# Flamingo kernel on one core: weight loads in another order, and the attentions' output bias added one tile at a time

## The chip, the core and the metric

The kernel runs on one core of a Trainium2 chip. The core has five engines that run at the same time, each with its own queue of instructions served in order: TensorE (PE in the profile; its weight loads are PEld), VectorE (DVE), ScalarE (ACT), GpSimd (POOL) and SyncE (SP), which here only issues DMAs. Engines wait for one another through semaphores. The metric is the device time of one execution in microseconds (us); lower is better.

## The reference

The input x has 2 batches of 2048 tokens with 512 features. A context of 2 x 128 tokens with 384 features is attended to. There are two layers, each a gated cross-attention and a gated feed-forward:

```python
def cross(x, y):                # 16 heads, over 128 context tokens
    q, k, v = proj(x), proj(y), proj(y)
    return softmax(q @ k.T * scale) @ v @ Wo + bo
x = x + tanh(g_xattn[0]) * cross0(layernorm(x), ctx)     # biased, inner width 512
x = x + tanh(g_ffn[0])   * routed(layernorm(x))
x = x + tanh(g_xattn[1]) * cross1(layernorm(x), ctx)     # inner width 1024
x = x + tanh(g_ffn[1])   * ternary_conv_ffn(layernorm(x))
```

`routed` picks the 256 tokens of each batch with the highest scores, runs causal attention and a SiLU-gated feed-forward of width 1365 on them, and writes them back. `ternary_conv_ffn` quantizes activations to integers and weights to -1, 0, 1, goes to width 2048, convolves over three neighbouring tokens, applies SiLU, quantizes again and projects back to 512.

## The kernel before

Everything is unrolled. The order of instructions on each engine is made by a planner: it takes the program's order as a priority and places what its own clock says is ready, so a later, ready instruction can pass an earlier one that waits. An instruction under `tc.keep_in_program_order` is kept where the program has it. Within a queue the order is then fixed, and an instruction that waits holds all behind it.

**Start.** ScalarE's queue issues the loads of bk, the first four x tiles (`load_x(0, nc.scalar)`, L989) and bq. SP's queue issues, in `load_context` (L160 to L168), the context ctxT, the key weights wk, the query weights wq, the value weights wv and bv, and then in `load_rest` (L172 to L174) the output weights wo and bias bo, which VectorE scales by the gate; then w_router and eight more x tiles. TensorE makes keys (L182) and values (L201), VectorE adds their biases (L191, L210), and then the first block's tokens are normalized (L104), transposed (L113) and projected to queries (L253).

**Stage 1** (L0 cross-attention) works on 8 blocks of 512 tokens. A block has 16 units, one head each: scores (L276), row maximum (L119, VectorE), exponent (L122, ScalarE), reciprocal (L130), the product with it (L131, POOL), transposes of the probabilities (L294), and values (L302) once per four heads. The output projection `back` of a block is cut into eight pieces, one per unit of the following block: a half of a tile's matmuls pp (L320), then the other half and L329, a VectorE operation that adds the gated pp to the residual tile and so frees pp's PSUM buffer. Ahead of the first piece POOL adds the bias bo to all four residual tiles (L316), so L329 need not wait for bias later. Beside the units run the router's scores and ranks (L810, L862, L906, VectorE).

**Stage 2** works on the selected tokens of one batch after the other: selected attention and then `feed_forward`, in 11 chunks of 128 columns. For each chunk SP loads w1c, w2c and w3c (L619 to L627), three chunks ahead, and TensorE makes pu, pw (L648) and acc (L633). Beside it weights are made ternary (`ternary`; L731 stores w2b). The second cross-attention's weights are loaded by the same `load_context` after the first batch's feed-forward in the program, and by `load_rest` in the third piece of the second batch's selected attention; its keys and values are made beside that attention.

**Stage 3** (L1 cross-attention) has 8 blocks of 16 units like stage 1 and runs beside the convolution of the blocks before: matmuls ph (L1159), POOL's small copies (L1169, L1171), VectorE's L1170, ScalarE's L1172 and two VectorE L1176 with two SBUF operands per slice. The end projects the quantized integers (L1389) and stores the output; the stores are issued on POOL's queue except those of the last block.

Of the kernel before, what the change touches and what calls it, by code (L numbers as in the profile page):

```python
# [17 lines left out]
P = 128  # L18
# [4 lines left out]
TB = BLK // P  # L23
# [7 lines left out]
NF = (DFF + P - 1) // P  # L31
# [7 lines left out]
def row_tiles(ap):  # L39
    return ap.rearrange("(c p) n -> p c n", p=P)  # L40
# [3 lines left out]
def flamingo_kernel(ctx: ExitStack, tc: tile.TileContext, a: dict, out: bass.AP):  # L44
    nc = tc.nc
# [4 lines left out]
    def psum_pool(stack, name, bufs):  # L50
        return stack.enter_context(tc.tile_pool(name=name, bufs=bufs, space=PSUM))
# [87 lines left out]
    class CrossWeights:  # L139
# [12 lines left out]
                self.bq = w.tile([P, nE], F32, name=L + "bq")  # L152
                self.bk = w.tile([P, nE], F32, name=L + "bk")

        def load_context(self, st, side):

            L, E = self.L, self.nE * P
            wkv = st.enter_context(tc.tile_pool(name=L + "wkv", bufs=1, side=side))
            self.ctxT = wkv.tile([P, CC, B * M], F32, name=L + "ctxT")
            nc.sync.dma_start(out=self.ctxT, in_=row_tiles(a["ctxT"]))  # L160
            self.wk = wkv.tile([P, CC, E], F32, name=L + "wk")
            nc.sync.dma_start(out=self.wk, in_=row_tiles(a[L + "WkT"]))
            nc.sync.dma_start(out=self.wq, in_=row_tiles(a[L + "WqT"]))
            self.wv = wkv.tile([P, CC, E], F32, name=L + "wv")
            nc.sync.dma_start(out=self.wv, in_=row_tiles(a[L + "WvT"]))
            if self.bias:
                self.bv = wkv.tile([P, E], F32, name=L + "bv")
                nc.sync.dma_start(out=self.bv, in_=a[L + "bv"].partition_broadcast(P))  # L168

        def load_rest(self):  # L170
            L = self.L
            nc.sync.dma_start(out=self.wo, in_=row_tiles(a[L + "WoT"]))  # L172
            nc.sync.dma_start(out=self.bo, in_=a[L + "bo"].partition_broadcast(P))
            nc.vector.tensor_scalar(self.bo, self.bo, self.g, None, ALU.mult)  # L174
# [40 lines left out]
    def cross_attention(  # L215
# [8 lines left out]
        L, nE, bias = W.L, W.nE, W.bias  # L224
        E = nE * P
# [86 lines left out]
        def back(n, residual, OT):  # L312

            tiles = residual()
            for t in tiles:
                tc.keep_in_program_order(nc.gpsimd.tensor_tensor(t, t, W.bo, ALU.add))  # L316
            for i, t in enumerate(tiles):
                pp = ps_mm.tile([P, D], F32, name="pp", tag="mm")
                for e in range(nE):
                    nc.tensor.matmul(  # L320
                        pp,
                        OT[e][:, ts(i, P)],
                        W.wo[:, e, :],
                        start=(e == 0),
                        stop=(e == nE - 1),
                    )
                    if e == nE // 2 - 1:
                        yield
                nc.vector.scalar_tensor_tensor(t, pp, W.g, t, ALU.mult, ALU.add)  # L329
                if i == TB - 1:  # L330
                    after_block(n, tiles)
                yield
# [10 lines left out]
        for U in range(N * H + 12):  # L343
            n, u = divmod(U, H)
            if n < N:
                grp, t = divmod(u, 4)
# [18 lines left out]
            if 0 <= V < N * H and V % 4 == 3:  # L365
                n, grp = divmod(V // 4, 4)
# [240 lines left out]
        yield from rms_rows(rows, g2, h2T[b], mm, pool)  # L607

    AHEAD = 3

    def feed_forward(b, ps_acc, mm, work):

        w13, gT = {}, {}
        acc = [ps_acc.tile([P, D], F32, name=f"acc{i}", tag=f"acc{i}") for i in range(2)]

        def load(f):
            n = min(P, DFF - f * P)
            w1c = wst.tile([P, DC, P], F32, name="w1c", tag="w1c")
            nc.sync.dma_start(  # L619
                out=w1c[:, :, :n], in_=row_tiles(a["W1T"])[:, :, ds(f * P, n)]  # L620
            )
            w2c = wst.tile([P, DC, P], F32, name="w2c", tag="w2c")
            nc.sync.dma_start(
                out=w2c[:, :, :n], in_=row_tiles(a["W2T"])[:, :, ds(f * P, n)]
            )
            w3c = wst.tile([P, D], F32, name="w3c", tag="w3c")
            nc.sync.dma_start(out=w3c[:n, :], in_=a["W3T"][ds(f * P, n), :])  # L627
            w13[f] = (w1c, w2c, w3c)

        def down(f):  # L630
            n = min(P, DFF - f * P)
            for i in range(2):
                nc.tensor.matmul(  # L633
                    acc[i],
                    gT[f][:n, ts(i, P)],
                    w13[f][2][:n, :],
                    start=(f == 0),
                    stop=(f == NF - 1),
                )

        for f in range(AHEAD):
            load(f)
        for f in range(NF):
            n = min(P, DFF - f * P)
            pu, pw = mm([P, CAP], "pu"), mm([P, CAP], "pw")
            for pt, wt in ((pu, w13[f][0]), (pw, w13[f][1])):
                for d in range(DC):
                    nc.tensor.matmul(  # L648
                        pt[:n, :],
                        wt[:, d, :n],  # L650
                        h2T[b][:, d, :],
                        start=(d == 0),
                        stop=(d == DC - 1),
                    )
            su = fact.tile([P, CAP], F32, name="su", tag="su")
            nc.scalar.activation(su[:n, :], pu[:n, :], AF.Silu)
            gT[f] = fact.tile([P, CAP], F32, name="gT", tag="gT")
            nc.vector.tensor_tensor(gT[f][:n, :], pw[:n, :], su[:n, :], ALU.mult)
            if f > 0:
                down(f - 1)  # L660
                if f - 1 + AHEAD < NF:
                    load(f - 1 + AHEAD)
            for w, n in work:
                for _ in range(n):
                    next(w, None)
        down(NF - 1)
        for w, _ in work:
            for _ in w:
                pass

        for i in range(2):
            t = xa[2 * b + i]
            nc.vector.tensor_tensor(t, acc[i], t, ALU.add)
            nc.vector.tensor_scalar(t, t, gf[0], None, ALU.mult)
            nc.gpsimd.indirect_dma_start(
                out=x_d[b][:, :],
                out_offset=bass.IndirectOffsetOnAxis(
                    ap=idx[:, 2 * b + i : 2 * b + i + 1], axis=0
                ),
                in_=t,  # L680
                in_offset=None,
                compute_op=ALU.add,
            )
# [61 lines left out]
    with ExitStack() as st:  # L745
# [16 lines left out]
            out=pick,  # L762
            in_=pick,
# [10 lines left out]
            out=after,  # L774
# [8 lines left out]
        def load_x(n, queue=nc.sync):  # L783
            if n < B * NBLK:
                for t in range(n * TB, (n + 1) * TB):
                    x[t] = xres.tile([P, D], F32, name="x", tag="x")
                    queue.dma_start(out=x[t], in_=x_in[t])
# [198 lines left out]
        sel_pools = selected_pools(st)  # L986
        W0 = CrossWeights("L0_", D // P, True, gx[0], st, "left")
        nc.scalar.dma_start(out=W0.bk, in_=a["L0_bk"])
        load_x(0, nc.scalar)  # L989
        nc.scalar.dma_start(out=W0.bq, in_=a["L0_bq"])  # L990
        with ExitStack() as st0:
            W0.load_context(st0, "left")
            W0.load_rest()
            nc.sync.dma_start(out=w_router, in_=a["w_router"].partition_broadcast(P))
            nc.vector.tensor_reduce(w_sum, w_router, AX.X, ALU.add)
            for n in (1, 2):
                load_x(n)
            selected_constants()
            with ExitStack() as st1:
                for _ in W0.keys_values(in_pool(psum_pool(st1, "L0_ps0", 2), "kv")):  # L1000
                    pass
# [41 lines left out]
    w4 = right.enter_context(tc.tile_pool(name="w4", bufs=1, side="right"))  # L1043
    w1q = w4.tile([P, DC, HID], BF16, name="w1q")
    W1 = CrossWeights("L1_", 1024 // P, False, gx[1], right1, "right")
    W1.load_context(right2, "right")
    with ExitStack() as sp:
        ps_o = psum_pool(sp, "s2b_o", 2)
        ps_sc = psum_pool(sp, "s2b_sc", 4)
        mm = in_pool(psum_pool(sp, "s2b_mm", 2), "mm")  # L1050
        second = selected_attention(
            1, mm, in_pool(ps_sc, "sc"), in_pool(ps_o, "o"), 4, selected_pools(sp), 2
        )
        keys_values = W1.keys_values(mm)
        for k, _ in enumerate(second):
            if k == 2:
                W1.load_rest()
            if k % 3 == 1:
                next(keys_values, None)
        for _ in keys_values:  # L1060
            pass
    with ExitStack() as sp:
        mm = in_pool(psum_pool(sp, "s2c_mm", 6), "mm")
        raw = raw_pools(sp)
        feed_forward(1, psum_pool(sp, "s2c_acc", 1), mm, [(ternary(0, mm, *raw), 1)])
    nc.vector.tensor_scalar(finstep, step[:, 1:2], gf[1], None, ALU.mult)
    sf.close()
    s2.close()
# [454 lines left out]
```

## Time and profile before

| what | value |
|---|---|
| median of 3 runs | 1771.91 us (1771.09 to 1772.97) |
| the profiled execution | 1771.65 us |
| its span, first to last instruction | 1770.0 us |
| mean granted TensorE clock | 0.971 |
| TensorE busy, first stretch 30 to 550 us | 473.5 of 520 us |
| TensorE busy, stage 3, 780 to 1600 us | 783.4 of 820 us |
| first matmul starts at | 11.02 us |
| L316, bias adds on POOL | 64, 86.8 us together |
| L131, products on POOL | 256, 275.8 us together |

Rows of the list of waits read: engine, tile and line that waited, who ended the wait, us in total, times, longest. Rows of the timeline read: start, duration, engine, line, operation, out<-in, shape, count, and in brackets the engine's idle time before it and what ended it. Where several instructions are merged, the duration is that of the row. Rows of the windows read: the stretch, its length, the busy time of PE, PEld, DVE, ACT and POOL with counts, the granted TensorE clock, the DMA engines' busy share and GB/s.

### The profile page before, as it was taken

Reading aid. Unit: us, or ns where it says so; the run is one execution under the profiler, and the core shown is the slowest. Engines: PE = TensorE matmul, PEld = TensorE weight load, DVE = VectorE, ACT = ScalarE, POOL = GpSimd, SP = SyncE. Lnnn points to the kernel's source line nnn. Section 1 sums busy time; section 2 is a strip of 40 time slices with the busy share of each in tenths; the row PEclk is TensorE's granted clock in tenths of the full one; section 3 lists DMA queues with packets and bytes.
Section 4 is the critical chain, followed back from the end, with each engine's and each line's share of the span. In section 5 each row is a group of like instructions: output and inputs, shape, how many; then the busy total and the mean of one; then the engine's idle time right before and its main releaser. Section 6 shows DMA issues by size and latency. Waiting matters only on the chain.

```text
span 1770.0 us, 25204 instructions
## 1 busy us (share of the span) xinstructions
PE 1642.2 (93%) x8076; PEld 863.0 (49%) x8122; DVE 1251.5 (71%) x2576; ACT 1101.4 (62%) x3170; POOL 556.4 (31%) x703
## 2 busy tenths in 40 slices
PE   6999889989999988999999999999999999989988
PEld 3544444445555655755454544545444454434433
DVE  4566877865757543345358888799788878877986
ACT  2876566456563323435367878778777787765575
POOL 2534443442440021023224242242423424233121
PEclk9999999999899989999999999999999999989999
DMA  6021112121006870730011334234143233247384
GB/s 218 7 67 55 36 61 66 51 75 54 25 36 207 286 241 25 229 87 25 19 54 72 109 110 146 90 114 155 42 158 117 84 104 118 88 161 269 135 305 153
DMA packets 116171, 196.98 MB, mean 111 GB/s; under 512 B 13084, under 2 KB 50716, under 8 KB 112328
## 3 DMA queue, kind: packets, MB, share of 16 engines
q1 hardware_dynamic: 109288, 176.50, 29.2%
q0 software_dynamic: 5888, 17.83, 3.2%
q8 instruction: 64, 1.05, 0.2%
q10 hardware_dynamic: 864, 1.05, 0.2%
q14 instruction: 67, 0.55, 0.1%
HBM read 120.89 MB, written 74.45 MB: 110 GB/s over the span
## 4 chain that ended last, share of the span: by engine, by line
PE 28%; DVE 18%; ACT 4%; DMA 3%; issue 2%; POOL 1%; SPq 0%; DVEq 0%; POOLq 0%; ACTq 0%
PE pq L253 8%; PE pp L320 7%; DVE h L1176 5%; PE po L302 3%; PE sc L276 3%; PE ph L1159 3%; PE tp L294 2%; DVE u L1170 2%; DVE nmx L119 1%; PE po L1389 1%; DVE AT L295 1%; DMA hf<-h_d 1%; DVE hf L1259 1%; ACT A L122 1%; DVE h L1209 1%
## 5 line engine op out<-in xcount | busy, mean ns | idle before, releaser
L122 ACT ACTIVATE A<-sc,nmx 128x128 f32<-128x128 f32 x1024 | 363.8, 385 | 130.1 <-DVE nmx L119 121.0
L131 POOL TENSOR_TENSOR A<-A,rden 128x512 f32<-128x512 f32 x256 | 275.8, 1079 | 510.2 <-DVE rden L130 407.6
L320 PE MATMUL pp<-L_wo,OT 128*128 128x512 f32 x768 | 367.0, 609 | 11.8 <-DVE x L329 11.7
L253 PE MATMUL pq<-xnT,L_wq 128*128 128x512 f32 x768 | 347.2, 600 | 12.1 <-DVE x L329 12.1
L122 ACT ACTIVATION_READ_ACCUMULATOR A<-sc,nmx 128x1 f32 x1024 | 229.5, 224 | 0.0
L253 PEld LDWEIGHTS pq<-xnT,L_wq 128*128 128x128 f32 x768 | 143.4, 192 | 172.7 <-issue 152.1
L119 DVE TENSOR_REDUCE nmx<-sc 128x4 f32<-128x512 f32 x256 | 168.6, 678 | 74.4 <-PE sc L276 74.3
L320 PEld LDWEIGHTS pp<-L_wo,OT 128*128 128x128 f32 x768 | 136.5, 193 | 157.6 <-issue 133.2
L1176 DVE SCALAR_TENSOR_TENSOR h<-u,cw,h 128x512 f32<-128x512 f32 x256 | 206.1, 838 | 6.1 <-ACT h L1172 5.6
L294 PE MATMUL tp<-ident,A 128*128 128x128 f32 x1024 | 164.7, 285 | 19.1 <-POOL A L131 13.9
L294 PEld LDWEIGHTS tp<-ident,A 128*128 128x128 f32 x1024 | 118.9, 143 | 88.3 <-issue 41.0
L295 DVE COPY AT<-tp 128x512 f32<-128x512 f32 x192 | 129.7, 677 | 44.4 <-PE tp L294 43.9
L276 PEld LDWEIGHTS sc<-L_kT,qT 32*128 32x128 f32 (+1 forms) x2048 | 110.7, 193 | 72.1 <-issue 60.3
L1172 ACT ACTIVATE h<-u,cb,cw 128x512 f32<-128x512 f32 x128 | 99.2, 808 | 68.6 <-DVE u L1170 57.5
L276 PE MATMUL sc<-L_kT,qT 32*128 32x128 f32 (+1 forms) x2048 | 136.9, 294 | 4.0 <-ACT A L122 3.4
L302 PE MATMUL po<-AT,L_v 128*32 128x512 f32 (+1 forms) x512 | 121.6, 667 | 11.5 <-DVE AT L295 11.0
L1159 PE MATMUL ph<-xiT,w1q 128*128 128x512 bf16 x477 | 122.7, 379 | 4.1 <-DVE u L1170 2.2
L1389 PE MATMUL po<-w2q,hq 128*128 128x512 bf16 x501 | 116.6, 380 | 9.3 <-ACT hq L1369 5.1
L1170 DVE TENSOR_TENSOR u<-ph,inv_b 128x512 f32<-128x512 f32 x128 | 85.4, 683 | 32.4 <-PE ph L1159 28.3
L130 DVE RECIPROCAL rden<-den 128x4 f32<-128x4 f32 x256 | 43.2, 169 | 80.2 <-ACT A L122 73.0
L1169 POOL COPY u<-carry 128x2 f32<-128x2 f32 x112 | 42.8, 384 | 147.0 <-DVE h L1176 121.8
L1159 PEld LDWEIGHTS <-w1q 128*128 128x128 bf16 x512 | 49.2, 98 | 81.2 <-issue 37.6
(246 smaller groups left out, 2389.2 us busy)
## 6 DMA issues: line engine op xcount, KB each, us to landing
h_d<-h SPq DMA_DIRECT2D x28, 1024.0 KB, 3.9
x_d<-x SPq DMA_DIRECT2D x64, 256.0 KB, 2.0
hf<-h_d SPq DMA_DIRECT2D x64, 256.0 KB, 3.2
x<-h_d SPq DMA_DIRECT2D x48, 256.0 KB, 4.7
x_d<-xo SPq DMA_DIRECT2D x32, 256.0 KB, 2.5
xf<-x_d SPq DMA_DIRECT2D x32, 256.0 KB, 3.1
x<-x_d SPq DMA_DIRECT2D x32, 256.0 KB, 3.0
hq_d<-hi SPq DMA_DIRECT2D x64, 128.0 KB, 1.8
```

What stands on the lines that cost most here:

```text
L119: nc.vector.tensor_reduce(nmx, sc, AX.X, ALU.max, negate=True)
L122: nc.scalar.activation(out_tile[:, h, :], sc[:, h, :], AF.Exp, bias=nmx[:, h : h + 1], accum_out=den[:, h : h + 1],)
L131: nc.gpsimd.tensor_tensor(out_tile, out_tile, rden.unsqueeze(2).to_broadcast([P, n, width]), ALU.mult,)
L253: nc.tensor.matmul(pq, W.wq[:, d, ts(e, P)], xnT[:, d, :], start=(d == 0), stop=(d == DC - 1),)
L276: nc.tensor.matmul(sc[h][:, t, :], qT[e % cpg][r, ts(t, P)], W.kT[r, b, e, :], start=True, stop=True,)
L294: nc.tensor.transpose(tp[:, t, :], A[:, t, :], ident)
L295: copy(AT, tp.rearrange("p t n -> p (t n)"))
L302: nc.tensor.matmul(po[h * dh : (h + 1) * dh, :], W.v[:, b, ts(hd, dh)], AT[c * hpc + h], start=True, stop=True,)
L320: nc.tensor.matmul(pp, OT[e][:, ts(i, P)], W.wo[:, e, :], start=(e == 0), stop=(e == nE - 1),)
L1159: nc.tensor.matmul(ph, w1q[:, d, ts(c, P)], xiT[g][:, d, :], start=(d == 0), stop=(d == DC - 1),)
L1176: nc.vector.scalar_tensor_tensor(z, u[:, ds(k, BLK)], cw[:, c, k : k + 1], z, ALU.mult, ALU.add)
L1389: nc.tensor.matmul(po, rows(c), w2q[:, c, :], start=(c == 0), stop=(c == HC - 1))
```

## The change

In both cross-attentions `load_context` and `load_rest` become one generator, `load_keys`, with two stops. It issues ctxT and wk, wk in two halves; then wv; then wq, bv, wo and bo. For layer 0 the first four x tiles are loaded on SP's queue between the second part and the third, no longer on ScalarE's. For layer 1 each part is tied by `issue_after` to a load of the feed-forward on SP's queue, and can't be issued ahead of it: ctxT and wk behind w3c of batch 0's last but one chunk, wv behind that of its last chunk, the rest behind w3c of batch 1's chunk 5 (counted from 0). In `back` the bias is added to the first tile at the front, and to tile i+1 after the stop in the middle of tile i's matmuls.

```diff
-        def load_context(self, st, side):
+        def load_keys(self, st, side):
             self.ctxT = wkv.tile([P, CC, B * M], F32, name=L + "ctxT")
             nc.sync.dma_start(out=self.ctxT, in_=row_tiles(a["ctxT"]))
             self.wk = wkv.tile([P, CC, E], F32, name=L + "wk")
-            nc.sync.dma_start(out=self.wk, in_=row_tiles(a[L + "WkT"]))
-            nc.sync.dma_start(out=self.wq, in_=row_tiles(a[L + "WqT"]))
+            for k in range(2):
+                half = ts(k, E // 2)
+                nc.sync.dma_start(
+                    out=self.wk[:, :, half], in_=row_tiles(a[L + "WkT"])[:, :, half]
+                )
+            yield
             self.wv = wkv.tile([P, CC, E], F32, name=L + "wv")
             nc.sync.dma_start(out=self.wv, in_=row_tiles(a[L + "WvT"]))
+            yield
+            nc.sync.dma_start(out=self.wq, in_=row_tiles(a[L + "WqT"]))
...
-        def load_rest(self):
-            L = self.L
             nc.sync.dma_start(out=self.wo, in_=row_tiles(a[L + "WoT"]))
...
             tiles = residual()
-            for t in tiles:
+            def add_bias(i):
+                t = tiles[i]
                 tc.keep_in_program_order(nc.gpsimd.tensor_tensor(t, t, W.bo, ALU.add))
+            add_bias(0)
             for i, t in enumerate(tiles):
...
                     if e == nE // 2 - 1:
                         yield
+                        if i + 1 < TB:
+                            add_bias(i + 1)
...
+            issued[b, f] = nc.sync.dma_start(out=w3c[:n, :], in_=a["W3T"][ds(f * P, n), :]).ins
...
-        load_x(0, nc.scalar)
...
-            W0.load_context(st0, "left")
-            W0.load_rest()
+            loads = W0.load_keys(st0, "left")
+            next(loads)
+            next(loads)
+            load_x(0)
+            for _ in loads:
+                pass
...
-    W1.load_context(right2, "right")
+    loads = W1.load_keys(right2, "right")
+    with tc.issue_after(issued[0, NF - 2]):
+        next(loads)
...
-            if k == 2:
-                W1.load_rest()
+            if k == 0:
+                with tc.issue_after(issued[0, NF - 1]):
+                    next(loads)
...
         feed_forward(1, psum_pool(sp, "s2c_acc", 1), mm, [(ternary(0, mm, *raw), 1)])
+    with tc.issue_after(issued[1, 5]):
+        for _ in loads:
+            pass
```

More of the change, by code (lines that the diff above doesn't have):

```diff
@@ L609, in flamingo_kernel @@
     AHEAD = 3
+    issued = {}
     def feed_forward(b, ps_acc, mm, work):
@@ L626, in load @@
             w3c = wst.tile([P, D], F32, name="w3c", tag="w3c")
-            nc.sync.dma_start(out=w3c[:n, :], in_=a["W3T"][ds(f * P, n), :])
+            issued[b, f] = nc.sync.dma_start(out=w3c[:n, :], in_=a["W3T"][ds(f * P, n), :]).ins
             w13[f] = (w1c, w2c, w3c)
```

## Prediction

> **What bounds the kernel now.** I read the list of waits first, then the timeline where a wait touches TensorE, then windows.
>
> ```profile
> PE 1642.2 (93%) x8076; PEld 863.0 (49%) x8122; DVE 1251.5 (71%) x2576; ACT 1101.4 (62%) x3170; POOL 556.4 (31%) x703
> PE pq L253 <- DVE x L329: 12.1, 7, 2.3
> PE pp L320 <- DVE x L329: 11.7, 4, 6.0
> PE acc L633 <- DMA w3c<-in_W3T: 4.3, 1, 4.3
> ```
>
> TensorE is the bound, so only idle TensorE time and slow clock can be won. Three idle places are touched by the change: the 11.02 us before the first matmul, the 4.3 us for w3c, and 23.8 us (11 waits) for L329, the VectorE add that frees pp's PSUM buffer. L329 itself is ready late, and the timeline of one stage-3 block shows why (POOL's rows first, then DVE's, PE's):
>
> ```profile
> 1048.92 1.04 POOL L131 TENSOR_TENSOR A<-A,rden 128x512 f32<-128x512 f32 x1
> 1049.92 5.60 POOL L316 TENSOR_TENSOR x<-x,L_bo 128x512 f32<-128x512 f32 x4
> 1055.45 1.32 POOL L1171 COPY carry<-u 128x2 f32<-128x2 f32 x2
> ...
> 1051.40 1.76 DVE L1259 TENSOR_TENSOR hf<-hf,s_b 128x512 f32<-128x512 f32 x1
> 1054.28 3.77 DVE L1176 SCALAR_TENSOR_TENSOR h<-u,cw,h 128x512 f32<-128x512 f32 x4
> 1057.97 0.74 DVE L329 SCALAR_TENSOR_TENSOR x<-pp,gate,x 128x512 f32<-128x512 f32 x1
> ...
> 1058.77 3.70 PE L253 MATMUL pq<-xnT,L_wq 128*128 128x512 f32 x8 [1.85 <-DVE x L329]
> ```
>
> While POOL runs its four bias adds in a row, VectorE's operations with two SBUF operands stretch: L1259 to 1.76 us (0.68 beside an idle POOL), four L1176 to 3.77 (2.65). One L1176 took 5.42 us, the longest of 256 with a median of 0.74. L329 is late and TensorE stands for 1.85 us.
>
> **The change, part by part.**
>
> *Bias adds, stages 1 and 3.* Nothing is added or removed: 64 adds, 86.8 us of POOL. Three of each four move from the front of `back` to later units, one at a time. From the timeline I took, for each of the 16 groups, what VectorE's operations took above their median beside an idle POOL, and the TensorE wait that follows. Stage 1, groups at 134, 187, 251 and 464 us: lost 2.9, 5.1, 3.1, 4.0, waits 2.3, 6.0, 3.0, 1.3; the other four lost 3.8, 0.9, 0 and 0 and are not followed by a wait that an earlier VectorE would shorten. Stage 3, seven groups from 941 (the one at 844 lost nothing): lost 1.8, 2.4, 2.2, 1.6, 2.2, 2.6, 4.7, waits 1.8, 1.8, 2.0, 1.2, 1.8, 2.3, 1.8 (the last for L1170, late with it). One add stays in place, so I count three quarters of the loss, capped by the wait: 2.2+3.8+2.3+1.3 = 9.6 in stage 1, 1.4+1.8+1.7+1.2+1.7+1.9+1.8 = 11.5 in stage 3, 21.1 in all. The 6.0 us wait at 192 is followed by a pp matmul of 1.22 us instead of 0.59, so its slow clock goes too: +3.
>
> Against it, the 48 moved adds (48 x 1.28 = 61 us) meet VectorE elsewhere. The Trainium skill's SBUF page ("Who interferes with whom") says that a VectorE instruction with two SBUF inputs and a GpSimd instruction that reads SBUF exclude each other for the whole instruction. That speaks against this change: spreading leaves the locked time as it is, and if each moved add costs VectorE as much as now (37 us, the losses' sum, in 86.8 us of adds: 0.43 per us), 61 x 0.43 = 26 and the gain is gone. The nearest row is L131, the same kind of operation, which is already spread: over stage 3 it costs VectorE 21 us in 138, 0.15 per us. I take the row: 61 x 0.15 = 9.2 us of VectorE, of which I let half reach TensorE, -4.6. Then 21.1 + 3 - 4.6 = 19.5. VectorE is 78% busy in stage 3 and often takes over as the next limit, so I let 70% through: **-14**. Bounds: -24 (no new meeting) and +3 (all meet L1176).
>
> The moved adds bring a wait: L329 of tile i+1 now needs an add issued one unit after the group's start. It comes two units later (7 us in stage 1, where L329 ran at 84.7, 91.8 and 99.2), so I cost it at nothing. Queued behind an add on POOL are L1171, L1169 and the next L131; ScalarE's L1172 waits for the second, the transposes L294 for the third. Stage 3's 128 units last 6.4 us each (780 to 1600 us) and POOL is busy for 2.2 of them (276 of 820 us); that slack hides an add; without it, each costs 1.28.
>
> *First loads.* Before, ctxT, wk, wq, wv went out on SP while four x tiles (1 MB) went out on ACT's queue; the first key matmul waited for wk.
>
> ```profile
> 11.02 4.50 PE L182 MATMUL pk<-L_ctxT,L_wk 128*128 128x256 f32 x12 [11.02 <-DMA L_wk<-in_L_WkT]
> 24.92 1.90 DVE L104 TENSOR_SCALAR xn<-x,L_ln_mv,L_ln_rstd 128x512 f32<-128x512 f32 x4
> 29.54 1.22 PE L253 MATMUL pq<-xnT,L_wq 128*128 128x512 f32 x1
> ```
>
> Now x waits behind ctxT, wk (two halves) and wv. ctxT and wk are 1.15 MB; at the 181 to 223 GB/s that all queues moved in the first 11 us they are in by 6 to 7 us, and the first half earlier. I start TensorE at 6.5, -4.5. Keys and values keep their 4.50+2.86+5.31 us. Then TensorE stood 1.88 for xn; x0 and wq end at 3.9 MB, by the 384 GB/s of 11 to 30 us near 15 to 18, so xn may come in time. But the value add L210 now needs bv, issued behind wq, and VectorE serves in order: if normalizing stands behind it, or behind the bo scaling (bo landed at 20.9), xn is later. I take 0.5 of the 1.88: **-5**; bounds -8.5 and 0. One more SP issue and four moved to SP cost about 0.45 each there, before anything is late.
>
> *Second attention's keys, values and weights, end of feed-forward 0.*
>
> ```profile
> 608.04 0.45 SPq L163 DMA_DIRECT2D L_wq<-in_L_WqT  x1
> 609.81 1.55 SPq L731 DMA_DIRECT2D w_d<-w2b  x2
> 611.46 0.34 SPq L627 DMA_DIRECT2D w3c<-in_W3T  x1
> ...
> 621.89 2.81 PE L633 MATMUL acc<-w3c,gT 85*128 85x512 f32 x3 [4.31 <-DMA w3c<-in_W3T]
> ...
> 617.50:621.90 4.40, 0.09 (x2) 0.04 (x1) 0.88 (x2) 0.00 (x0) 0.00 (x0) 1.00 1.04 337
> 621.90:632.30 10.40, 9.41 (x21) 5.56 (x22) 4.51 (x9) 0.00 (x0) 1.68 (x1) 0.51 1.05 346
> ```
>
> The last w3c sat behind 2 MB of wq on the SP queue and landed after 10 us; in the windows the number after the five engines' busy times is the granted clock: after the stop, 9.41 us of matmuls ran at 0.51. wq now goes out much later, and only ctxT and wk (1.9 MB, 6 us at 314 GB/s) follow the last but one w3c at 602.1, drained near 609 with the stores between; w3c lands near 615, before TensorE asks at 617.5. So 4.31 plus half of 9.41 go: 9.0. The Trainium skill's TensorE page ("What's actually happening") gives one window of about 3.4 us at half clock after an idle one, which would make 4.31 + 1.7 = 6.0; the clock row is longer and I take it, less 1 us for w1c and w2c of the last chunk, now behind wk: **-8**, bounds -9 and -3. The next wait (wv of the second selection, held at 620.46 by w2b's stores) moves earlier too, since those stores no longer queue behind wq; L_wv (1.5 MB) issues beside it, first needed at 673.
>
> *wq, wo, bo behind chunk 5 of feed-forward 1.* They pass to after w3c at 724.8: 2+2+0.25 MB, three SP issues. At 346 to 384 GB/s that is 11 to 12 us, to about 737. SP issues w2c of chunk 6 at 725.19, asked for at 736.9, w1c of chunk 7 at 726.5, asked for at 740.3: if wq overtakes w2c, TensorE waits up to 2.5 us. TensorE is busy for 62.0 of 62 us there, so nothing hides it: **+1**, bounds 0 and +5 (with slow clock). wq is needed at 764.5, wo at 840: in time.
>
> **Sum.** 1771.65 (profiled execution; span 1770.0) - 14 - 5 - 8 + 1 = 1745.65, **1746**. That execution is 0.3 below the median shown.
>
> **Rivals.**
> 1. *Only the loads gain.* The moved adds meet VectorE as often as before (the lock rule above): 1771.65 - 12 = 1760. For: stage 3's VectorE has L1176 in every unit. Against: L131, right before, costs half per us.
> 2. *The stop moves instead of going.* FFN 1 waits 5 us for chunk 6, and x0 behind wv takes the start's gain: 1771.65 - 14 - 8 + 5 = 1755. For: 4.25 MB before chunks with 10 us of lead. Against: the lead nearly suffices.
> 3. *Slower: adds on POOL's path.* In stages 1 and 3 a moved add stands before L131 or L1169 and holds the transposes or ScalarE by 1.28. With 32 of 48 on the path: +41, against -26 of the parts together, 1787; from 21 on the gain is eaten. For: TensorE already waits for L131 13.9 us in 16 places. Against: the four adds in a row cause none of these.
> 4. *The adds stay together*, since the order within POOL is a planner's: 1760, as rival 1.
>
> **How the numbers follow.** Forecast 0.55 (own range 1734 to 1755), rivals 1 and 4 together 0.20, rival 2 0.13, rival 3 0.12. 0.2% is 3.5 us, about what a measurement of this kernel can tell. Slower takes rival 3 but its lightest end, 0.11; same 0.06 from the ends of rivals 1 and 3; faster 0.83. The range 1732 to 1768 leaves out rival 3 and some 0.06 below.
>
> **What would show it.** Right: L316's groups of four gone from POOL's timeline; L1176's mean below 0.80 us (0.838 now), its longest below 2.5; waits for L329 under 10 us; no w3c wait, clock near 1 in the 10 us after it; first matmul near 6.5 and first pq near 24.5; feed-forward 1 without a wait. Wrong: waits on POOL's L131 or L1169 grow, or a w1c or w2c wait appears near 735.

## The result, and the profile after

The changed kernel takes 1742.43 us (median of 4, 1737.58 to 1744.60) against 1772.44 us before (median of 4): a ratio of 0.9826 with a 95% interval of 0.9803 to 0.9849, 30 us shorter. The forecast was 1746. Its profiled execution took 1741.68 us with a span of 1740.0. Between the two profiled executions TensorE's idle time falls by 16.6 us and its busy time, for the same 8076 matmuls, by 13.4, at a mean granted clock of 0.982 after 0.971. Several us of that busy time are scatter between executions: a kernel that hardly differs from the one before (wq alone moved, below) has 1636.0 us of it, where the kernel before has 1642.2.

The page's busy times and the list of TensorE's waits, kernel after (L316 of before is now L322, L329 is L339, L1176 is L1196, L253 is L256, L320 is L328; for the waits: who waited, who ended it, us in total, times, longest):

```profile
PE 1628.8 (94%) x8076; PEld 856.4 (49%) x8122; DVE 1240.6 (71%) x2576; ACT 1103.3 (63%) x3170; POOL 560.1 (32%) x703
```

```profile
PE pp L328 <- DVE x L339: 5.4, 3, 2.6
PE tp L297 <- DVE cnt L937: 4.9, 2, 3.2
...
PE pq L256 <- DVE x L339: 1.2, 2, 1.0
```

The waits for the add that frees pp fell from 23.8 us in 11 to 6.6 us in 5, and the wait for w3c is gone from the list. A wait that the kernel before did not have stands in their place, 4.9 us for L937 (cnt). VectorE does the same 2576 instructions in 10.9 us less.

The timeline of one block in stage 3, kernel after (POOL's rows first, then VectorE's; start, duration, engine, line):

```profile
1031.56 1.27 POOL L322 TENSOR_TENSOR x<-x,L_bo 128x512 f32<-128x512 f32 x1
1039.45 1.27 POOL L322 TENSOR_TENSOR x<-x,L_bo 128x512 f32<-128x512 f32 x1
...
1034.84 2.73 DVE L1196 SCALAR_TENSOR_TENSOR h<-u,cw,h 128x512 f32<-128x512 f32 x4
1037.49 0.74 DVE L339 SCALAR_TENSOR_TENSOR x<-pp,gate,x 128x512 f32<-128x512 f32 x1
```

The adds stand alone, eight microseconds apart. Four L1196 take 2.73 us here; the four shown before took 3.77. L339 comes right behind them, and TensorE doesn't wait.

The start, timeline of TensorE, kernel after:

```profile
5.98 6.83 PE L185 MATMUL pk<-L_ctxT,L_wk 128*128 128x256 f32 x18 [5.98 <-DMA L_wk<-in_L_WkT]
14.27 1.56 PE L185 MATMUL pk<-L_ctxT,L_wk 128*128 128x256 f32 x6 [1.46 <-DVE L_kT L194]
15.91 5.42 PE L204 MATMUL pv<-L_wv,L_ctxT 128*128 128x512 f32 x12
22.80 1.30 PE L113 MATMUL ptr<-ident,xn 128*128 128x128 f32 x6 [1.47 <-issue]
...
27.31 1.22 PE L256 MATMUL pq<-xnT,L_wq 128*128 128x512 f32 x1
```

Keys begin 5.04 us earlier, but the first query matmul only 2.23 us earlier: a wait for VectorE's kT, which frees the keys' PSUM, has come up at 14.27. VectorE's timeline shows why kT is late:

```profile
8.91 0.48 DVE L194 TENSOR_SCALAR L_kT<-pk,L_bk 128x256 f32<-128x256 f32 x1 [4.38 <-PE pk L185]
...
13.13 0.69 DVE L99 BATCH_NORM_STATS2 L_ln_st<-x 128x6 f32<-128x512 f32 x1 [3.60 <-DMA x<-in_x]
13.74 0.47 DVE L194 TENSOR_SCALAR L_kT<-pk,L_bk 128x256 f32<-128x256 f32 x1
```

The first three key groups were done at 12.81, but the second kT stands on VectorE's queue behind L99, the statistics of the first x tile, and L99 waited 3.60 us for x, which now comes behind the weights.

The end of feed-forward 0, kernel after: SP's queue and TensorE's last down projection from the timeline, then the windows (length, busy time of PE, PEld, DVE, ACT and POOL, granted clock, DMA share, GB/s):

```profile
598.60 0.43 SPq L164 DMA_DIRECT2D L_wk<-in_L_WkT  x1
599.12 0.44 SPq L638 DMA_DIRECT2D w3c<-in_W3T  x1
599.61 0.40 SPq L164 DMA_DIRECT2D L_wk<-in_L_WkT  x1
...
603.64 2.97 SPq L169 DMA_DIRECT2D L_wv<-in_L_WvT  x1
...
606.26 3.60 PE L644 MATMUL acc<-w3c,gT 128*128 128x512 f32 x8
```

```profile
604.50:613.00 8.50, 7.38 (x28) 4.17 (x26) 3.17 (x7) 0.38 (x1) 1.69 (x1) 1.00 1.06 385
613.00:623.00 10.00, 9.68 (x30) 5.41 (x31) 2.03 (x5) 1.17 (x2) 1.56 (x1) 1.00 1.07 310
```

The last w3c is issued between the two halves of wk and ahead of L_wv, TensorE doesn't wait for it, and the clock stays at 1.00.

**Where the 30 us came from.** I matched VectorE's and ScalarE's instructions one to one between the two traces and took how much earlier each comes. The lead is 2.6 us at 40 to 80 us, 9.4 behind stage 1, 17.7 behind feed-forward 0, 18.3 behind feed-forward 1, about 33 at the end of stage 3 and 29.8 at the end. So: start 2.6, stage 1 about 7, end of feed-forward 0 about 8, stage 3 about 14, and some 3 us given back behind it.

### The profile page after: what moved, and what is told of

Same layout as the page of the kernel before. It is cut to its first block, busy times and chain, and to the rows that moved or that the text cites. A ratio compares the mean times of both kernels' runs of the same rounds, so it can differ in the third digit from the quotient of the medians.

```text
span 1740.0 us, 25223 instructions
## 1 busy us (share of the span) xinstructions
PE 1628.8 (94%) x8076; PEld 856.4 (49%) x8122; DVE 1240.6 (71%) x2576; ACT 1103.3 (63%) x3170; POOL 560.1 (32%) x703
## 4 chain that ended last, share of the span: by engine, by line
PE 48%; DVE 27%; ACT 9%; issue 6%; DMA 6%; POOL 3%; SPq 0%; DVEq 0%; POOLq 0%; ACTq 0%
PE pp L328 12%; PE pq L256 9%; DVE h L1196 4%; PE po L305 4%; PE tp L297 4%; PE sc L279 4%; ACT A L122 3%; PE ph L1179 3%; DVE nmx L119 2%; DVE marks L873 2%; DVE u L1190 2%; DVE AT L298 1%; DMA x<-h_d 1%; DVE L_ln_st L99 1%; DMA h_d<-h 1%
## 5 line engine op out<-in xcount | busy, mean ns | idle before, releaser
L131 POOL TENSOR_TENSOR A<-A,rden 128x512 f32<-128x512 f32 x256 | 280.5, 1098 | 493.9 <-DVE rden L130 402.4
L328 PE MATMUL pp<-L_wo,OT 128*128 128x512 f32 x768 | 360.8, 601 | 5.4 <-DVE x L339 5.4
L256 PE MATMUL pq<-xnT,L_wq 128*128 128x512 f32 x768 | 344.8, 596 | 1.3 <-DVE x L339 1.2
L256 PEld LDWEIGHTS pq<-xnT,L_wq 128*128 128x128 f32 x768 | 142.5, 191 | 159.7 <-issue 151.4
L328 PEld LDWEIGHTS pp<-L_wo,OT 128*128 128x128 f32 x768 | 134.9, 191 | 148.9 <-issue 130.9
L1196 DVE SCALAR_TENSOR_TENSOR h<-u,cw,h 128x512 f32<-128x512 f32 x256 | 197.2, 803 | 5.8 <-ACT h L1192 5.3
L305 PE MATMUL po<-AT,L_v 128*32 128x512 f32 (+1 forms) x512 | 120.1, 655 | 11.5 <-DVE AT L298 11.1
```

Source lines behind the costliest of these rows:

```text
L131: nc.gpsimd.tensor_tensor(out_tile, out_tile, rden.unsqueeze(2).to_broadcast([P, n, width]), ALU.mult,)
L256: nc.tensor.matmul(pq, W.wq[:, d, ts(e, P)], xnT[:, d, :], start=(d == 0), stop=(d == DC - 1),)
L305: nc.tensor.matmul(po[h * dh : (h + 1) * dh, :], W.v[:, b, ts(hd, dh)], AT[c * hpc + h], start=True, stop=True,)
L328: nc.tensor.matmul(pp, OT[e][:, ts(i, P)], W.wo[:, e, :], start=(e == 0), stop=(e == nE - 1),)
L1196: nc.vector.scalar_tensor_tensor(z, u[:, ds(k, BLK)], cw[:, c, k : k + 1], z, ALU.mult, ALU.add)
```

## The experiments

### The parts one at a time

Three kernels take one part of the change each, on the kernel before.

The adds alone:

```diff
-            for t in tiles:
+            def add_bias(i):
+                t = tiles[i]
                 tc.keep_in_program_order(nc.gpsimd.tensor_tensor(t, t, W.bo, ALU.add))
+            add_bias(0)
...
+                        if i + 1 < TB:
+                            add_bias(i + 1)
```

> Kernel before with the bias adds spread, one per tile, and nothing else of the change. Theory (what counted was the bunching of four adds ahead of L329, by the shift of TensorE's events in stages 1 and 3: 7.5 + 12.3 us): about 20 us shorter, 1752, and TensorE's waits for L329's successor fall from 23.8 us to about 7. Prediction on record: 14 shorter, 1758. Rival (only the loads gain): within 4 us of the kernel before, 1772.

Measured: 1756.76 us against 1772.49, ratio 0.9896 (0.9863 to 0.9929), 15.7 us by the medians. The waits for the add that frees pp fell to 6.9 us, and a wait for cnt of 4.9 us came up here too. The rival that only the loads gain falls.

The first attention's load order alone:

```diff
-        load_x(0, nc.scalar)
...
-            W0.load_context(st0, "left")
-            W0.load_rest()
+            loads = W0.load_keys(st0, "left")
+            next(loads)
+            next(loads)
+            load_x(0)
+            for _ in loads:
+                pass
```

> Kernel before with only the first attention's load order (keys' weights in two halves, values, then x, then wq). By the shift of the first query matmul in the changed kernel: 2 to 3 us shorter, 1770. By the prediction's own sum: 5 us shorter, 1767. Rival 2 (x behind wv takes the gain): no difference.

Measured: 1764.19 us, ratio 0.9947 (0.9928 to 0.9966), 8.3 us by the medians and 6 us at the interval's near end. That is more than either theory said. Its profiled execution was its longest (1777.12), so for the gain its trace is read for the start alone: first query matmul at 28.11, 1.4 us earlier than in the kernel before. Where the rest of the 8.3 us comes from, that trace can't say.

The second attention's loads alone:

```diff
-    W1.load_context(right2, "right")
+    loads = W1.load_keys(right2, "right")
+    with tc.issue_after(issued[0, NF - 2]):
+        next(loads)
...
-            if k == 2:
-                W1.load_rest()
+            if k == 0:
+                with tc.issue_after(issued[0, NF - 1]):
+                    next(loads)
...
+    with tc.issue_after(issued[1, 5]):
+        for _ in loads:
+            pass
```

> Kernel before with only the second attention's loads placed behind the last chunks of feed-forward 0 and behind chunk 5 of feed-forward 1. Theory: the 4.3 us stop for w3c and the half-speed stretch of 10 us after it go, 8 us shorter, 1764; if the half-speed stretch has another cause, 4 us shorter, 1768, with the clock still near 0.5 after 617 us.

Measured: 1765.93 us, ratio 0.9963 (0.9950 to 0.9976), 6.6 us by the medians. There is no w3c wait, and the windows show clock 1.00 in each stretch from 600 to 632 us. Between the matched instructions at 616 us, ahead of the stop, and at 633 us, behind it, its trace gains 8.3 us, and so do the seven other traces that have this part of the change. The half-speed stretch goes with the stop.

The medians of the three add up: 15.7 + 8.3 + 6.6 = 30.6, where the whole change gave 30.0. Each has an interval of some 2 to 6 us to each side, so a fit this close is in part luck.

### The start, taken out of the change

```diff
-            loads = W0.load_keys(st0, "left")
-            next(loads)
-            next(loads)
-            load_x(0)
-            for _ in loads:
-                pass
+            W0.load_context(st0, "left")
+            W0.load_rest()
```

(with `load_x(0, nc.scalar)` and `load_context` as before)

> Changed kernel with the first attention's loads put back to the order of before. The start alone measured 8 us on the kernel before, but its first query matmul moved by only 2 to 3. If the start is worth what its events show: 1745 (2.5 over the changed kernel). If it is worth 8, by a clock that is granted differently afterwards: 1750.

Measured: 1748.40 us, ratio 0.9875 (0.9850 to 0.9900); the changed kernel stands at 0.9826. That is 6.0 us by the medians, so the start is worth 6 to 8 by time. In the traces the first query matmul stands at 29.54 to 31.07 in seven profiled executions with the old order (mean 30.3) and at 27.27 to 29.54 in five with the new (mean 27.9): 2.3 us. By the matched instructions this kernel is 4.3 us behind the changed one from 40 us to 160 us and 3.0 at the end of stage 3. Traces and times differ by some 3 us; the intervals are 4 us to each side, so this stays open.

### Four PSUM buffers for the first keys and values

```diff
-                for _ in W0.keys_values(in_pool(psum_pool(st1, "L0_ps0", 2), "kv")):
+                for _ in W0.keys_values(in_pool(psum_pool(st1, "L0_ps0", 4), "kv")):
```

> Changed kernel with four instead of two PSUM buffers for the first attention's keys and values. If the start's missing gain is the third key group waiting for VectorE to free PSUM (1.46 us) and the value groups behind it: 1.5 to 4 us below the changed kernel, 1739, first query matmul near 25. If x's own path (normalizing behind the value adds on VectorE) sets the first query matmul: no difference, 1742, first query matmul near 27.3.

TensorE's timeline with four buffers:

```profile
5.97 8.10 PE L185 MATMUL pk<-L_ctxT,L_wk 128*128 128x256 f32 x24 [5.97 <-DMA L_wk<-in_L_WkT]
13.91 5.31 PE L204 MATMUL pv<-L_wv,L_ctxT 128*128 128x512 f32 x12
20.70 1.30 PE L113 MATMUL ptr<-ident,xn 128*128 128x128 f32 x6 [1.47 <-issue]
...
24.75 3.70 PE L256 MATMUL pq<-xnT,L_wq 128*128 128x512 f32 x8 [0.19 <-ACT xnT L245]
```

The wait of 1.46 us at 14.27 is gone, and the first query matmul comes at 24.75. VectorE still waits here for the first x tile (3.39 us), but TensorE no longer waits for VectorE. The time was 1740.67, so I ran it again beside the changed kernel on one chip:

> Changed kernel with four PSUM buffers for the first keys and values, beside the changed kernel on the same chip: its first query matmul came 2.6 us earlier (24.75 for 27.31). If that carries to the end: 2 to 4 us below the changed kernel; if later waits take it back: no difference.

> The changed kernel itself, on the same chip as the run with four PSUM buffers: 1742, 30 us below the kernel before.

Measured there: 1738.06 (ratio 0.9811, 0.9786 to 0.9836) against 1739.00 for the changed kernel (0.9824, 0.9800 to 0.9848). The first query matmul came at 25.43 against 29.54. So it is shown that TensorE was held because a keys' buffer came free late. That L99's wait for x made it late is read from the traces (all five new-order traces with two buffers show it, 3.5 to 4.7 us long); a kernel with kT ahead of L99 was not run. A gain at the end of the run is not shown.

### What made w3c late

Only wq is moved, behind everything else in the second attention's first loads:

```diff
-            nc.sync.dma_start(out=self.wq, in_=row_tiles(a[L + "WqT"]))
+            if self.bias:
+                nc.sync.dma_start(out=self.wq, in_=row_tiles(a[L + "WqT"]))
...
+            if not self.bias:
+                nc.sync.dma_start(out=self.wq, in_=row_tiles(a[L + "WqT"]))
```

> Kernel before with only the second attention's wq moved behind the last w3c of feed-forward 0 on the SP queue (wk whole, wv, ctxT and the rest as before). If wq's 2 MB ahead of w3c made the stop: no wait for w3c, clock near 1 after 617 us, as the whole move of the second attention's loads, 1766. If the order of wk and wv counts as well: the stop stays in part, 1769 to 1772.

Measured: 1771.88 us, ratio 0.9995 (0.9981 to 1.0010). No gain by time; its trace gains some 2 us at this place, which the interval (1.8 us longer to 3.4 shorter) can't tell from nothing. SP's queue and TensorE in its timeline, then its windows:

```profile
608.06 0.51 SPq L166 DMA_DIRECT2D L_wv<-in_L_WvT  x1
609.89 1.69 SPq L734 DMA_DIRECT2D w_d<-w2b  x2
611.67 0.38 SPq L630 DMA_DIRECT2D w3c<-in_W3T  x1
612.15 0.40 SPq L174 DMA_DIRECT2D L_wq<-in_L_WqT  x1
...
620.57 3.12 PE L636 MATMUL acc<-w3c,gT 85*128 85x512 f32 x4 [3.09 <-DMA w3c<-in_W3T]
```

```profile
617.50:620.57 3.07, 0.00 (x1) 0.03 (x1) 1.21 (x3) 0.00 (x0) 0.00 (x0) 1.00 1.03 296
620.57:631.00 10.43, 9.02 (x25) 5.47 (x26) 4.59 (x10) 0.00 (x0) 1.68 (x1) 0.67 1.06 363
```

L_wv was issued at 608.06 in the slot that L_wq had at 608.04. The last w3c went out at 611.67, as late as before (611.46), and TensorE waited 3.09 us instead of 4.31. So it wasn't wq as such: with wq moved, the next large load, wv, went out ahead of the last w3c. The changed kernel ties wv behind that w3c. Its ctxT and wk are tied one chunk earlier; ctxT and half of wk did go out ahead of the last w3c, and it still came in time.

### What a bias add costs: left out, or replaced by work that reads nothing

Four kernels leave the output bias out of both attentions. In two of them, one on each kernel, the adds are simply gone; in the other two GpSimd fills the bias tile with zeros instead, three fills for an add, in the same places. Fills write SBUF and read nothing from it, and they keep GpSimd busy somewhat longer (107 us for 86.8).

```diff
-            for t in tiles:
-                tc.keep_in_program_order(nc.gpsimd.tensor_tensor(t, t, W.bo, ALU.add))
```

> Kernel before with the output bias left out in both attentions (it is never added; 64 adds, 86.8 us of GpSimd, are gone). It bounds what the adds cost at all. Theory (what VectorE still loses to spread adds lies off the path): within 3 us of the run that only spreads them, about 1750. Rival (spread adds still cost by the lock, 0.27 per us of 61): 10 to 16 us shorter than the run that spreads them, about 1738.

```diff
-            for t in tiles:
-                tc.keep_in_program_order(nc.gpsimd.tensor_tensor(t, t, W.bo, ALU.add))
+            for _ in range(12):
+                tc.keep_in_program_order(nc.gpsimd.memset(W.bo, 0.0))
```

> Kernel before with each group of four bias adds replaced by twelve GpSimd memsets of the bias tile (the bias is not added; GpSimd is kept busy about as long in the same place and writes SBUF, but reads nothing from it). If the 31 us that leaving the adds out is worth come from VectorE being held while GpSimd reads SBUF: as without adds, 1741, with L1176's mean near 0.75 us. If they come from GpSimd being busy (its queue, what stands behind the adds): as before, 1772. The bias is left out.

```diff
-                t = tiles[i]
-                tc.keep_in_program_order(nc.gpsimd.tensor_tensor(t, t, W.bo, ALU.add))
+                for _ in range(3):
+                    tc.keep_in_program_order(nc.gpsimd.memset(W.bo, 0.0))
```

> Changed kernel with each spread bias add replaced by three GpSimd memsets of the bias tile (the bias is not added). Leaving the adds out of the kernel before was worth 31 us where spreading them was worth 16, the 15 of difference mostly in stage 1. If what the spread adds still cost is VectorE held: some 13 to 15 us below the changed kernel, 1728. If it is GpSimd's time ahead of L131 (the third rival, mild): as the changed kernel, 1742.

```diff
-                t = tiles[i]
-                tc.keep_in_program_order(nc.gpsimd.tensor_tensor(t, t, W.bo, ALU.add))
+                pass
```

> Changed kernel with the output bias left out in both attentions (never added, GpSimd neither reads nor writes for it). If the parts add: the kernel before lost 31 us by leaving the adds out, and the loads are worth some 14, so 1772 - 31 - 14 = 1727, 8 below the run with spread memsets (then GpSimd's time in between is worth 8 of the 15 that spread adds cost, VectorE held 7). If GpSimd's time costs nothing: as the spread memsets, 1735.

Times and ratios to the kernel before: no adds on the kernel before 1741.29 (0.9813, 0.9785 to 0.9842); fills in its groups 1744.19 (0.9852, 0.9819 to 0.9885); fills one tile at a time on the changed kernel 1735.25 (0.9793, 0.9763 to 0.9823); no adds on the changed kernel 1725.81 (0.9740, 0.9711 to 0.9769). No adds were to give 1750 by my theory, in which what spread adds still cost lies off the path: that theory falls.

The table takes the stages from the traces. Stage 1 lies between the instructions that stand at 105 and 545 us in the kernel before, stage 3 between those at 940 and 1600 (the lead of the matched instructions within 10 us of each end, good to about 1 us); idle is TensorE's; VectorE is the page's busy time over the whole span.

| kernel | adds | stage 1, us | idle | stage 3, us | idle | VectorE busy |
|---|---|---|---|---|---|---|
| before | in fours | 440.0 | 42.9 | 660.0 | 32.8 | 1251.5 |
| before, adds alone changed | one at a time | 434.9 | 42.5 | 648.8 | 24.5 | 1239.9 |
| after | one at a time | 433.4 | 42.9 | 645.6 | 22.5 | 1240.6 |
| after, run again | one at a time | 431.2 | 39.8 | 644.2 | 22.7 | 1240.9 |
| before, fills | fills in twelves | 426.0 | 36.0 | 641.9 | 21.4 | 1223.7 |
| after, fills | fills in threes | 428.7 | 36.8 | 641.1 | 21.1 | 1221.1 |
| before, no adds | none | 422.9 | 32.9 | 644.7 | 21.9 | 1219.1 |
| after, no adds | none | 422.5 | 32.6 | 641.2 | 20.9 | 1220.0 |

**It is the reading.** The timeline of the kernel before with fills, in the stage-3 block shown for the kernel before, which stands some 14 us earlier in that trace (POOL's row first):

```profile
1038.17 4.60 POOL L316 MEMSET L_bo<- 128x512 f32 x8
...
1039.31 2.72 DVE L1176 SCALAR_TENSOR_TENSOR h<-u,cw,h 128x512 f32<-128x512 f32 x4
```

Four L1176, wholly beside eight fills, take 2.72 us; beside the adds they took 3.77. Over the whole trace 26 L1176 lay 17.25 us beside fills and no other GpSimd work, and lost nothing (-0.03 us in sum). Adds in fours stretch VectorE by 1251.5 - 1219.1 = 32.4 us; fills in their place by 4.6. By time, the fills cost 2.9 us over no adds, where adds in fours cost 31.2. A fill also gives L329 nothing to wait for, where an add makes its operand; but the trace of the kernel before shows no wait of VectorE for L316, so that isn't the difference. What the bunched adds cost was VectorE held while GpSimd reads, not GpSimd being busy.

**Spreading saves in two different ways.** In stage 3 TensorE's idle time falls to 22.5 us, within 2 us of what is left with no adds at all: there the spread adds leave TensorE almost no wait more. In stage 1 the idle time is 42.9 us before and 42.9 after (39.8 when run again), though no adds give 32.9. Between these two traces stage 1 got shorter by TensorE's busy time, 397.1 to 390.5, and the windows show why (same columns as above; kernel before, then after):

```profile
180.00:300.00 120.00, 104.84 (x655) 52.92 (x653) 91.46 (x196) 73.93 (x305) 49.92 (x44) 0.94 0.16 54
```

```profile
180.00:300.00 120.00, 102.86 (x687) 52.99 (x682) 90.74 (x203) 75.28 (x308) 51.16 (x45) 0.99 0.15 54
```

The granted clock rose from 0.94 to 0.99; in the three other kernels with adds in fours it is 0.94 to 0.96 here, in the five other traces with spread adds 0.96 to 0.99. The one wait of 6.0 us at 198.02 became two, 2.58 us at 190.68 and 3.20 at 199.37. I did not isolate that from the other shortened waits.

The split into idle and busy time is luck of the two traces, though. Over three kernels with adds in fours (before, the second attention's loads alone, wq alone) and the six traces with spread adds, stage 1's mean length falls from 438.8 to 432.6 us: idle time from 44.0 to 40.7, busy time from 394.8 to 391.9, about half of the gain each.

**What stands behind a spread add in stage 1.** The new wait is for cnt. The timeline of POOL, VectorE and TensorE around it, kernel after, and TensorE's rows when it was run again:

```profile
191.12 1.27 POOL L322 TENSOR_TENSOR x<-x,L_bo 128x512 f32<-128x512 f32 x1
192.34 1.57 POOL L131 TENSOR_TENSOR A<-A,rden 128x512 f32<-128x512 f32 x1
193.87 1.02 POOL L90 TENSOR_TENSOR L_ln_rstd<-L_ln_rstd_e,neghalf 128x4 f32<-128x4 f32 x1
...
195.86 1.44 POOL L322 TENSOR_TENSOR x<-x,L_bo 128x512 f32<-128x512 f32 x1
...
194.93 3.57 DVE L104 TENSOR_SCALAR xn<-x,L_ln_mv,L_ln_rstd 128x512 f32<-128x512 f32 x4 [1.81 <-POOL L_ln_rstd L90]
...
198.57 0.65 DVE L937 TENSOR_TENSOR cnt<-new,cnt 64x512 f32<-64x512 f32 x1
...
190.68 1.98 PE L328 MATMUL pp<-L_wo,OT 128*128 128x512 f32 x4 [2.58 <-DVE x L339]
199.37 1.09 PE L297 MATMUL tp<-ident,A 128*128 128x128 f32 x4 [3.20 <-DVE cnt L937]
```

```profile
193.94 3.47 PE L328 MATMUL pp<-L_wo,OT 128*128 128x512 f32 x4 [2.58 <-DVE x L339]
202.62 0.63 PE L297 MATMUL tp<-ident,A 128*128 128x128 f32 x4 [1.71 <-DVE cnt L937]
```

From pp to the transposes tp it is 8.7 us in both traces, set by VectorE: the less TensorE waits for cnt, the longer its matmuls ahead took. So the length of a stage says more than its idle time. A moved add stands on POOL ahead of L131 and L90 (the standard deviations of the next block); VectorE's L104 waits 1.81 us for L90, is then stretched by the next add and an L131, and cnt stands behind it. In the changed kernel with no adds the same place reads:

```profile
190.72 1.38 POOL L90 TENSOR_TENSOR L_ln_rstd<-L_ln_rstd_e,neghalf 128x4 f32<-128x4 f32 x1
...
192.13 2.63 DVE L104 TENSOR_SCALAR xn<-x,L_ln_mv,L_ln_rstd 128x512 f32<-128x512 f32 x4 [0.80 <-POOL L_ln_rstd L90]
```

L104 waits 1.0 us less and runs 0.94 us shorter; from pp to tp it is 6.9 us, and TensorE's wait for cnt is 1.45 us. So a wait for cnt is left even without adds; the spread adds lengthen this place by 1.8 us. Spread fills, which don't read, leave stage 1 at 428.7, 6.2 us above no adds, and TensorE's waits for cnt at 4.8 us. So of the 9 to 11 us that spread adds still cost in stage 1, about 6 go with GpSimd's time ahead of what VectorE needs (somewhat less, since three fills take longer than an add), and 3 to 5 with its reading. By time, spread fills cost 9.4 us over no adds, and adds 4 to 7 over fills; the intervals are some 5 us to each side, so the first is just clear of them and the second is not. Against my expectation that fills would fall to 1728, GpSimd's time is the larger share. Which of the queued instructions carry it over the whole stage, I did not trace beyond this one place.

## Why the prediction was right, and where not

**The time and the sum.** The forecast of 1746 missed by 4 us. Predicted were adds -14, start -5, feed-forward 0 -8, feed-forward 1 +1; the kernels with one part each measured 15.7, 8.3 and 6.6 shorter (the last with feed-forward 1 in it). That the sum came so near is in part luck: within the adds too much was expected of stage 1 and too little of stage 3.

**Bias adds, the mechanism: right.** Bunched adds hold VectorE's two-operand operations, L329 is late and TensorE stops; 21.1 us of waits, nearly all for L329, were to go, and L329's waits fell by 17.2. L1196's mean fell to 803 ns (forecast below 0.80 us, a hair off), its longest to 1.76 us (below 2.5), and the waits to 6.6 (below 10).

**The rule against the row.** The Trainium skill's page "SBUF — State Buffer" ("Who interferes with whom") was read as saying that spreading leaves the locked time as it is. The page's lock itself is borne out: reads hold a two-operand VectorE instruction, writes alone don't, as the fills show. But how much is locked depends on what VectorE runs beside the add. VectorE's loss fell from 32.4 us to 1240.6 - 1220.0 = 20.6. If a quarter of 32.4, 8.1 us, stayed with the adds in place, the 64 us of moved adds cost 12.5: 0.20 per us. I took 0.15 from L131's row; the rule with the present loss was 0.43. The row was the better guide.

**Where the gain lies: mis-sized both ways.** The sum gave stage 1 (9.6 + 3 less a share) somewhat more than stage 3 (11.5). By the matched instructions it was 5 to 9 us in stage 1 and 11 to 16 in stage 3. The failed step for stage 3 is the discount: half of the moved adds' VectorE time on the path and 70% let through, where idle TensorE time fell by 8 to 10 of the 11 us that no adds at all would give. For stage 1 the failed step is the one that cost at nothing what is queued behind a moved add. It named these instructions on POOL, but computed the slack for stage 3 only. In stage 1 the waits for L329 fell by about 7 us, but idle time fell by 3 on the mean of the traces where 9.6, less the discounts, was forecast, and the busy time, where the clock shows, by another 3, as the sum had it. What kept the rest is the third rival's mechanism in part, at about 6 us in one stage instead of 41.

**Start: size near, working wrong.** The first matmul came at 5.98 (6.5 forecast), the first query matmul at 27.31 (24.5). The step let keys and values keep their durations and asked of x only whether it comes in time for normalizing. It does, but VectorE serves L99, which needs x, ahead of the second kT: x, at 13.13 instead of 5.02 behind wk and wv, held kT, kT held one of the keys' two PSUM buffers, and TensorE waited. That is the second rival's second half, taking some 2.5 of the 5 us. With four buffers the first query matmul came at 24.75. The fear for xn behind bv's add was half right: normalizing stood behind the value adds. By time the start gave 6 to 8, of which the traces account for 2 to 4; the rest is open, so that the time came near -5 is no proof of the step.

**End of feed-forward 0: right by size and clock, wrong by name.** 8.3 us in the traces for 8. The half-clock row made it 9.0 less 1, the rule of one window of 3.4 us (Trainium skill, "TensorE: Matmul & The Clock Gate", "What's actually happening") 6.0. Measured 6.6 by time (4.3 to 8.9), 8.3 in each of eight traces: nearer to the row, though the time alone doesn't exclude the rule. The step said that w3c sat behind wq. With wq moved away it sat behind wv, and moving wq alone gained nothing by time.

**Feed-forward 1: +1 forecast, nothing seen.** The trace of the changed kernel is 0.6 us shorter there; the eight traces with this part lie from 1.0 shorter to 1.3 longer, those without it from 0.9 shorter to 2.0 longer. wq went out at 708.25, behind the w3c of 705.93, which answers to the 724.8 of before, as forecast. But wo followed at 718.83 and bo at 728.89, each with the w3c loads of further chunks between, so no chunk had to compete with more than 2 MB at a time, and TensorE waits for no load there. The step had all three go out together.

## What to carry to other kernels

GpSimd work that reads SBUF is best counted by what VectorE runs beside it and by who stands behind VectorE: four adds in a row ahead of the instruction that frees a PSUM buffer cost a TensorE stop, the same four spread out nearly none in stage 3, as long as the spread adds don't stand ahead of something short that VectorE waits for on GpSimd's own queue. A late small load is cured by tying the large loads behind it, not by moving one large load, since the next one takes its slot. When an early load starts TensorE sooner, ask whether the consumer of its PSUM buffers keeps up, and what that consumer's queue waits for ahead of it: here a load that had been moved back.

## What the runs showed of the hardware that was not expected

The fills, which read nothing, left two-operand VectorE instructions alone but did slow some with one SBUF operand: seven L862 (128x512, 476 ns alone) lost 2.15 us in 4.85 us beside fills on the kernel before, where the fills took 0.68 us instead of 0.52, and four L104 lost 1.12 in 2.61 beside fills on the changed kernel. With reading adds, two L104 lost 1.88 us in 2.40, and six L1196 lost 5.33 us in 6.49. An instruction that reads its other operand from PSUM lost nothing: five L1170, 0.04 us in 3.56 beside the adds of the kernel before. A TensorE stop of 3.09 us was followed by 10.43 us at a mean clock of 0.67, where a stop of 4.31 was followed by 10.40 at 0.51.
